# A GRU with a mixture of experts behind it: where the first block's gate inputs are summed, how the first seeds reach the gates, which engine adds the biases, and when zeros are copied

## The chip, the cores and the metric

The kernel runs on one core of a Trainium2 chip. The metric is the device time of one execution in microseconds. A core has five engines with queues of their own: TensorE (PE for its matmuls, PEld for its weight loads), VectorE (DVE), ScalarE (ACT), GpSimd (POOL) and SyncE (SP, which issues DMAs here). Each engine takes its instructions in program order; engines wait for one another, and for DMAs, by semaphores.

## The reference

The input x is [8, 256, 512], eight sequences of 256 steps. A GRU cell with a state of 512 goes over the steps, and a mixture of experts with a shared expert works on its outputs; x is added at the end. All in float32.

```python
def cell(h, x):
    gi = x @ W_ih + b_ih
    gh = h @ W_hh + b_hh
    i_r, i_z, i_n = jnp.split(gi, 3, axis=-1)
    h_r, h_z, h_n = jnp.split(gh, 3, axis=-1)
    r = jax.nn.sigmoid(i_r + h_r)
    z = jax.nn.sigmoid(i_z + h_z)
    n = jnp.tanh(i_n + r * h_n)
    h_new = (1.0 - z) * n + z * h
    return (h_new, h_new)
...
combine = jnp.sum(topk_w[..., None] * jax.nn.one_hot(topk_ids, E, dtype=x.dtype), axis=1)
gu = jnp.einsum('th,ehf->etf', x, w_gate_up)
act = _silu_and_mul(gu)
eo = jnp.einsum('eti,eih->eth', act, w_down)
routed = jnp.einsum('te,eth->th', combine, eo)
shared = _silu_and_mul(x @ w_sh_gate_up) @ w_sh_down
return (routed + shared).reshape(orig_shape)
```

There are 8 experts of width 256, of which each token takes 2, and the shared expert has a width of 1024.

## The kernel before

**Blocks and chunks.** The 256 steps are cut into 16 blocks of 16 steps (TS); a block holds 128 rows, 8 sequences by 16 steps. A block is cut into chunks of 4 steps (SC).

**The projections.** For block k and gate g (0 is r, 1 is z, 2 is n) `project(k, g)` makes four pieces, one for each quarter q of the contraction with W_ih. A piece is four matmuls with 512 columns each, which the trace shows as eight records of L338, `gip<-we,xT`. The sum of a gate stands in one PSUM bank. There are three such banks (`ps_mm`, handed out by `bank_of`), used in turn by projections, routing and the shared expert; whoever takes a bank first makes its old readers run, if they still stand in a queue (`held`). After the last piece `end()` brings the sum, plus the bias, into the tile `gi`. For block 0 one VectorE instruction does that (L430) into `gi_first`. For all other blocks ScalarE copies the bank into `gi_later` (L432) and GpSimd adds the bias there (L433). `gi_later` is a single tile with room for three gates of one block, so a gate's copy for block k+1 waits until the DMA that sends block k's values has read them. After gate z, the r and z columns are sent to DRAM (`gid_rz`, L441); after gate n, the n columns (`gid_n`, L443). Both sends are issued by SP. The sends of block 0 (`send_first`, L457 and L459, one for each chunk and kind) are issued by ACT.

**The seeds.** `load_seeds(c)` (L475) reads a chunk's gate inputs back from DRAM into `seeds` (r and z) and `seeds_n`, with partitions laid out as the gates need them; there are two buffers of each. `open_gate(n, g)` (L486, ACT) copies one step's seeds into the PSUM bank of the gate (`banks`, `gate_of`), and the recurrent matmuls add to it there. Chunk 0 is read by eight loads, four on ACT and four on POOL; every later chunk by eight loads on SP, issued after the last step of the chunk before the one that runs.

**A step.** `step(n)` issues the matmuls of r and n (32 records of L514 on `ps_rn`), then of z (32 on `ps_z`). VectorE turns r and n (L527), ACT takes the sigmoid of r (L531) and opens the next step's r and n gates, VectorE multiplies and adds (L534, L535), ACT takes the tanh (L537) and the sigmoid of z (L539) and opens the next z gate, VectorE forms the new state hT (L542, L544, L545), and ACT copies it to `hc` (L548). POOL copies one column of `hn` (L543); the next step's `hn` waits for that. Step n+1's matmuls need step n's hT and the opened gates.

**Between the steps.** Matmul work of other kinds is cut into pieces and put behind the matmuls of each step: projections of later blocks, the shared expert (`shared_unit`), routing. Each step may take 8 units of it (`PER_STEP`), a unit being four matmuls with 128 columns, or half of four with 256; what the routing uses is taken off. VectorE work of 0.66 to 1.1 us by the planner's own cost figures is put in a queue, `afterwards`, with its cost: the turn of a block's x (`transpose_x`, 1.1, L327), the shared expert's product (`weighted`, 0.9, L769 and L770), its final sum (`add_up`, 0.66). After each step `catch_up(room)` takes items from the front while their cost fits in the room: `WINDOW`, 1.1, less what the step's routing takes on VectorE (`busy` in the table `steps_`). If a consumer comes first, `needed()` runs every item up to the wanted one.

The routing of block k-1 runs in block k: `order_experts` in its step 2 (busy 1.2), `weigh` in 4 (1.0), `give_places` in 6 (1.2), `send_rows` in 8 (0.75, eight DMAs `rows<-hr` on SP), `read_rows` in 10 (`rb<-rows` on SP), each one step later in block 1, where `weigh_all` takes another 0.7 in step 6. The dealing of rows to experts (`deal_rows`, indirect DMAs on POOL) follows in steps 12 and 14. The DRAM tile `dealt` must hold zeros where no row is dealt: SP copies `blank` to it, eight DMAs of 256 KB in each block, one in each of steps 2 to 9.

**The head.** x_0 and three quarters of W_ih are queued on SP, then the two biases, the last quarter of W_ih, x_1, W_hh, x_2. TensorE turns x_0 (`turn_x_plain`), projects block 0 quarter by quarter over the three gates, turns x_1, runs ten pieces of block 1, and then step 0 is issued. POOL, after its constants, copies the hidden bias of n into both `seeds_n` tiles (L296).

**The tail.** After the 256 steps the rest of the shared expert and the experts' tiles run.

Of the kernel before, what the change touches and what calls it, by code (L numbers as in the profile page):

```python
# [17 lines left out]
P = 128  # L18
TS = 16
SC = 4  # L20
NS = 2
NH = 4


@with_exitstack
def kernel(
# [109 lines left out]
    for q in range(NQ):  # L136
        if q == NQ - 1:
            nc.sync.dma_start(bias, b_ih.partition_broadcast(P))
            nc.sync.dma_start(bias_h, b_hh[0 : 2 * D].partition_broadcast(P))
        nc.sync.dma_start(wih[:, q], w_ih.rearrange("(p q) n -> q p n", q=NQ)[q])  # L140
    load_x_plain(1)
    w_hh_v = w_hh.rearrange("(q p) n -> p q n", p=P)
# [147 lines left out]
    for j in range(4):  # L290
# [3 lines left out]
        )  # L294
    for tile_ in seeds_n:
        nc.gpsimd.tensor_copy(tile_, seed_hn.unsqueeze(1).broadcast_to([P, SC, P]))  # L296

# [12 lines left out]
    blank = dram.tile([P, D], F32, name="blank")  # L310
    load((dealt[E * NM], nothing), (blank, nothing))


# [91 lines left out]
    def project(k, g):  # L405

        box = {}

        def issue(q, cols):
            if q == 0 and cols.start == 0:  # L410
                if k in turned_x:
                    turned_x.pop(k)()
                box["ps"], _ = bank_of([P, D], f"gip_{k}_{g}")
            multiply(
                box["ps"][:, cols],
                lambda c: xT_of[k][:, c, q, :],
                wih[:, q, g * D + cols.start : g * D + cols.stop],
                start=(q == 0 and cols.start == 0),
                stop=(q == NQ - 1 and cols.stop == D),
            )  # L420

        def by_group(t_):
            return t_.rearrange("p (q j i) -> p j q i", q=NQ, j=4)

        def end():
            gi = gi_later if k else gi_first
            to_gi = gi[:, :, g, :].rearrange("p j (q i) -> p j q i", q=NQ)
            bias_g = by_group(bias[:, g * D : (g + 1) * D])
            if k == 0:
                nc.vector.tensor_tensor(to_gi, by_group(box["ps"]), bias_g, ALU.add)  # L430
            else:
                nc.scalar.copy(to_gi, by_group(box["ps"]))  # L432
                nc.gpsimd.tensor_tensor(to_gi, to_gi, bias_g, ALU.add)  # L433
            if g > 0:
                projected.add((k, "rzn"[g]))
            if g > 0 and k == 0:
                send_first(g, 0)
            elif g > 0:
                to = gi_dram[k][g % 2].rearrange("j b t n -> (b t) j n")
                if g == 1:  # L440
                    nc.sync.dma_start(to.rearrange("p j (a n) -> p j a n", a=2), gi[:, :, 0:2, :])  # L441
                else:
                    nc.sync.dma_start(to, gi[:, :, 2, :])  # L443

        return [
            matmul_piece(lambda cols, q=q: issue(q, cols), end if q == NQ - 1 else None)
            for q in range(NQ)
        ]

    projected = set()  # L450

    def send_first(g, c):
# [3 lines left out]
        if g == 1:  # L456
            nc.scalar.dma_start(to.rearrange("p j (a n) -> p j a n", a=2), gi_first[rows_, :, 0:2, :])  # L457
        else:
            nc.scalar.dma_start(to, gi_first[rows_, :, 2, :])  # L459

    def load_seeds(c, of="nz"):

        k, o = divmod(c * SC, TS)
        steps = slice(o, o + SC)
        for g in of:
            assert (k, g) in projected
            tile_, at_row = (seeds_n[c % NS], B) if g == "n" else (seeds[c % NS], 0)
            for j in range(4):
                if k:
                    src = gi_dram[k][int(g != "n")][j, :, steps, :]  # L470
                else:
                    src = gi_first_dram[int(g != "n")][o // SC, j].rearrange("t b n -> b t n")
                by = nc.sync if c else nc.scalar if g == "z" else nc.gpsimd
                row = 32 * j + at_row
                by.dma_start(tile_[row : row + B], src)  # L475

# [492 lines left out]
    nc.vector.transpose(states[0].rearrange("p q b -> p (q b)"), h.rearrange("p q i -> p (q i)"))  # L969
    nc.vector.tensor_tensor(bias[:, 0 : 2 * D], bias[:, 0 : 2 * D], bias_h, ALU.add)  # L970

    first = [project(0, g) for g in range(3)]
    for q in range(NQ):
        for g in range(3):
            first[g][q].run(None)
    catch_up(None)
    load_seeds(0, "z")
    load_seeds(0, "n")
    load_shared()

    projections = deque()
    for k in range(1, NB):
        for g in range(3):
# [6 lines left out]
    def turn_x_afterwards(k):  # L990
        turned_x[k] = afterward(1.1, lambda: transpose_x(k))

    turn_x_plain(1)
    ahead_of_it = 2 * NQ + 2
    while ahead_of_it:
        piece = projections.popleft()
        ahead_of_it -= piece.parts > 0
        piece.run(None)
    for g in gate_of:
        open_gate(0, g)  # L1000
    for c in range(1, TS // SC):
        for g in (1, 2):
            send_first(g, c)
    load_seeds(1)
    due = spent = 0.0
    to_enter = deque()
    for k in range(NB):
# [21 lines left out]
        for e in range(E):  # L1029
            when(2 + e, 0, 0, lambda k=k, e=e: nc.sync.dma_start(dealt[e * NM + k], blank))  # L1030
        if k > 1 and k % 2:
# [126 lines left out]
```

## Time and profile before

| what | us |
|---|---|
| median of 3 runs | 1397.16 |
| lowest, highest | 1394.51, 1398.63 |
| the profiled execution | 1394.11 |
| its span in the trace | 1391.9 |
| first matmul of step 0 | 32.07 |
| first matmul of step 1 | 37.76 |
| last step's matmuls | near 1141 |
| x is turned for block 1 on TensorE | 19.70 |
| bias sums on POOL (L433), 45 of them | 1.27 each |
| bias sums on VectorE for block 0 (L430), 3 | 0.69 each |
| VectorE turn of a block's x (L327), 14 | 1.15 each |

In the profile a line of the timeline has the start in us, the duration, engine, line, operation, what it writes and reads, and how often; in brackets is the idle time of its engine before it and what ended that. Lines of a waits view give who waited for whom, with us in total, times, and the longest. A q behind an engine's name means its sequencer, which issues DMAs.

### The profile page before, as it was taken

Reading aid. Unit: us, or ns where it says so; the run is one execution under the profiler, and the core shown is the slowest. Engines: PE = TensorE matmul, PEld = TensorE weight load, DVE = VectorE, ACT = ScalarE, POOL = GpSimd, SP = SyncE. Lnnn points to the kernel's source line nnn. Section 1 sums busy time; section 2 is a strip of 40 time slices with the busy share of each in tenths; the row PEclk is TensorE's granted clock in tenths of the full one; section 3 lists DMA queues with packets and bytes.
Section 4 is the critical chain, followed back from the end, with each engine's and each line's share of the span. In section 5 each row is a group of like instructions: output and inputs, shape, how many; then the busy total and the mean of one; then the engine's idle time right before and its main releaser. Section 6 shows DMA issues by size and latency. Waiting matters only on the chain. (4 is left out here: it accounts for less than half of the span.)

```text
span 1391.9 us, 58971 instructions
## 1 busy us (share of the span) xinstructions
PE 1369.2 (98%) x24512; PEld 781.5 (56%) x24512; DVE 653.6 (47%) x2701; ACT 473.5 (34%) x2037; POOL 291.2 (21%) x564
## 2 busy tenths in 40 slices
PE   8999999999999999999999999999999999999996
PEld 3455556665656565656665566566656655444442
DVE  2445444545454544455544554554445443344442
ACT  0444443434343434343434343434343330111111
POOL 3333432121111111111111111111111132133332
PEclk9999999999999999999999999999999999999999
DMA  8544563332332232223221322132223445455553
GB/s 269 169 138 147 125 125 108 112 107 90 97 100 67 74 83 75 67 82 83 81 76 59 83 83 82 59 87 78 67 67 90 127 112 154 91 93 102 94 102 50
DMA packets 94082, 137.62 MB, mean 99 GB/s; under 512 B 17256, under 2 KB 67864, under 8 KB 91768
## 3 DMA queue, kind: packets, MB, share of 16 engines
q1 hardware_dynamic: 77192, 95.54, 23.7%
q0 software_dynamic: 15152, 37.38, 11.8%
q8 instruction: 194, 3.18, 1.0%
q10 hardware_dynamic: 1472, 0.93, 0.3%
q14 instruction: 72, 0.59, 0.1%
HBM read 94.55 MB, written 72.78 MB: 120 GB/s over the span
## 5 line engine op out<-in xcount | busy, mean ns | idle before, releaser
L514 PE MATMUL ps_rn<-we,hT 128*8 128x256 f32 x8192 | 490.5, 379 | 5.6 <-DVE hT L545 2.7
L514 PEld LDWEIGHTS ps_rn<-we,hT 128*8 128x8 f32 x8192 | 223.3, 89 | 254.5 <-ACT ps_z L486 50.9
L527 DVE STREAM_TRANSPOSE rT<-ps_rn 128x128 f32<-128x128 f32 x256 | 81.1, 317 | 435.2 <-PE ps_rn L514 435.2
L514 PE MATMUL ps_z<-we,hT 128*8 128x128 f32 x8192 | 272.2, 273 | 0.0
L514 PEld LDWEIGHTS ps_z<-we,hT 128*8 128x8 f32 x8192 | 227.4, 90 | 50.8
L531 ACT ACTIVATE rT<-rT 128x32 f32<-128x32 f32 x256 | 58.5, 229 | 527.7 <-DVE rT L527 519.7
L543 POOL COPY last_hn<-hn 128x1 f32<-128x1 f32 x256 | 47.3, 185 | 825.6 <-DVE hn L542 825.6
L824 PE MATMUL gu_s<-hc,wsu 128*32 128x256 f32 x3072 | 188.4, 379 | 0.0
L338 PE MATMUL gip<-we,xT 128*32 128x512 f32 (+2 forms) x1872 | 185.7, 520 | 1.9 <-DVE xT L220 1.6
L824 PEld LDWEIGHTS gu_s<-hc,wsu 128*32 128x32 f32 x3072 | 101.0, 110 | 58.7 <-issue 11.8
L778 PE MATMUL gu_t<-we,xrT 128*128 x280 | 131.6, 593 | 1.8 <-issue 1.8
L338 PE MATMUL po<-wsd,act_s 128*32 128x512 f32 (+2 forms) x1272 | 130.2, 509 | 0.0
L338 PEld LDWEIGHTS gip<-we,xT 128*32 128x32 f32 x1872 | 59.7, 111 | 71.4 <-issue 60.4
L778 PEld LDWEIGHTS gu_t<-we,xrT 128*128 128x128 f32 x280 | 50.5, 190 | 52.9 <-issue 45.0
L527 DVE STREAM_TRANSPOSE zT<-ps_z 128x128 f32<-128x128 f32 x256 | 78.9, 308 | 0.0
L548 ACT COPY hc<-hT 128x32 f32<-128x32 f32 x192 | 47.4, 247 | 91.2 <-DVE hT L545 90.7
L486 ACT COPY ps_rn<-seeds_n 128x128 f32<-128x128 f32 x256 | 69.0, 270 | 8.2
L534 DVE TENSOR_TENSOR rT<-nT,rT 128x32 f32<-128x32 f32 x256 | 50.0, 195 | 42.6 <-ACT rT L531 42.2
L527 DVE STREAM_TRANSPOSE nT<-ps_rn 128x128 f32<-128x128 f32 x256 | 70.0, 273 | 0.0
L486 ACT COPY ps_rn<-seeds 128x128 f32<-128x128 f32 x256 | 68.9, 269 | 2.1 <-DMA seeds<-gid_rz_first 1.0
L914 DVE TENSOR_SCALAR y<-yp,share 128x512 f32<-128x512 f32 x35 | 26.2, 750 | 91.8 <-PE yp L911 72.8
L542 DVE TENSOR_TENSOR hn<-hT,rT 128x32 f32<-128x32 f32 x256 | 49.3, 193 | 38.7 <-ACT rT L537 11.2
(167 smaller groups left out, 1188.5 us busy)
## 6 DMA issues: line engine op xcount, KB each, us to landing
dealt<-blank SPq DMA_DIRECT2D x128, 256.0 KB
xr<-dealt SPq DMA_DIRECT2D x140, 64.0 KB
we<-in_L_ffn_w_gate_up_dram POOLq DMA_DIRECT2D x32, 256.0 KB, 4.4
gid_rz<-gi SPq DMA_DIRECT2D x15, 512.0 KB
seeds<-gid_rz SPq DMA_DIRECT2D x240, 32.0 KB
wsu<-_L_ffn_w_sh_gate_up_dram POOLq DMA_DIRECT2D x16, 256.0 KB, 3.8
rows<-hr SPq DMA_DIRECT2D x128, 32.0 KB
rb<-rows SPq DMA_DIRECT2D x16, 256.0 KB
```

Source lines behind the costliest of these rows:

```text
L338: nc.tensor.matmul(ps[32 * c : 32 * c + 32], lhs(c), rhs, start=start, stop=stop, skip_group_check=True,)
L486: nc.scalar.copy(gate_of[g], src)
L514: nc.tensor.matmul(banks[g][32 * j : 32 * j + B, 0 : n_ * P].rearrange("b (a k i) -> b a k i", a=n_, k=NQ), hT[:, q, 0:B], whh_v[:, q, j, ...
L527: nc.vector.transpose(gT.rearrange("p a b -> p (a b)"), gate_of[g])
L531: nc.scalar.activation(r, r, AF.Sigmoid)
L534: nc.vector.tensor_tensor(r, nT[:, :, 0:B], r, ALU.mult)
L542: nc.vector.tensor_tensor(hn, hT[:, :, 0:B], nn, ALU.subtract)
L543: nc.gpsimd.tensor_copy(last_hn, hn[:, 0, 0:1])
L548: nc.scalar.copy(hc_of_block(k).rearrange("p g q (c t) -> p q g c t", t=TS)[:, :, :, :, t], new.rearrange("p q (g c) -> p q g c", c=2),)
L778: nc.tensor.matmul(box["ps"], lhs(q), w_up(q), start=(q == 0), stop=(q == NQ - 1))
L824: nc.tensor.matmul(box["ps"][32 * g : 32 * g + 32, two_i, :], wsu[c][:, q, two_i, fs], hc_of[m][:, :, q, :], start=(two_i == 0 and q == 0) ...
L914: nc.vector.tensor_scalar(y, box["y"], laid["share"][:, i : i + 1], None, ALU.mult)
```

## The change

- Block 0's gate sums are built in the three gate banks (`rn`, `z`, `x`) in place of three of the `ps_mm` banks. VectorE still adds the bias into `gi_first`.
- Steps 0 and 1 (`NP = 2`) no longer get their seeds through DRAM. `pick`, a matrix of zeros and ones made by POOL from `ident`, picks their rows out of `gi_first` by 16 matmuls into the gate banks (`pick_seeds`, `first_seeds`); ACT copies r and z into `seeds[0]`, VectorE adds the hidden bias of n into `seeds_n[0]`.
- Steps 2 and 3 are still read back from DRAM. All eight sends of block 0 and these eight loads are issued by POOL, together, right after block 0's last projections.
- In the head, x_1 is loaded ahead of the biases and the last quarter of W_ih. The order on TensorE is: three quarters of block 0, turn of x_1, three quarters of block 1's r, last quarter of block 0, three quarters of block 1's z, the picks, block 1's last r quarter, three quarters of its n. The two pieces left over go to the front of the queue of the steps. POOL's copies into `seeds_n` come after its zeros and `pick`.
- For blocks 1 to 15 the bias is added by VectorE instead of POOL, and not at once: the sum is put in `afterwards` at a cost of 0.66, and the sends to DRAM go out when it runs. Before a gate's copy, a pending sum of the same gate is run.
- `turn_x_afterwards` rotates the queue by one, so that the turn of x comes to the front.
- The zero copies of a block move from steps 2 to 9 to pairs: two in each of steps 0, 1, 4 and 5 (in block 0: 4, 5, 8 and 9).

```diff
@@ -19,6 +19,7 @@
 TS = 16
 SC = 4
 NS = 2
+NP = 2
 NH = 4
 
 
@@ -135,10 +136,10 @@
     load_x_plain(0)
     for q in range(NQ):
         if q == NQ - 1:
+            load_x_plain(1)
             nc.sync.dma_start(bias, b_ih.partition_broadcast(P))
             nc.sync.dma_start(bias_h, b_hh[0 : 2 * D].partition_broadcast(P))
         nc.sync.dma_start(wih[:, q], w_ih.rearrange("(p q) n -> q p n", q=NQ)[q])
-    load_x_plain(1)
     w_hh_v = w_hh.rearrange("(q p) n -> p q n", p=P)
     for g in (0, 2, 1):
         cols = slice(g * D, (g + 1) * D)
@@ -292,8 +293,6 @@
             seed_hn[32 * j : 32 * j + B].rearrange("b (q i) -> b q i", q=NQ),
             b_hn[j].partition_broadcast(B),
         )
-    for tile_ in seeds_n:
-        nc.gpsimd.tensor_copy(tile_, seed_hn.unsqueeze(1).broadcast_to([P, SC, P]))
 
 
     rows = dram.tile([B, T, D], F32, name="rows")
@@ -309,6 +308,13 @@
     load((listed[0:P], vacant), (listed[P : E * NM + 1], vacant[0 : E * NM + 1 - P]))
     blank = dram.tile([P, D], F32, name="blank")
     load((dealt[E * NM], nothing), (blank, nothing))
+    pick = we[0 : SC * B, 2, 3, 0 : 6 * SC * B].rearrange("p (s m) -> p s m", s=SC)
+    nc.gpsimd.memset(pick, 0.0)
+    nc.gpsimd.tensor_copy(
+        pick[:, :, 2 * B : 3 * B], ident[0 : SC * B, 0 : SC * B].rearrange("p (s b) -> p s b", s=SC)
+    )
+    for tile_ in seeds_n:
+        nc.gpsimd.tensor_copy(tile_, seed_hn.unsqueeze(1).broadcast_to([P, SC, P]))
 
 
     spare = deque()
@@ -410,7 +416,10 @@
             if q == 0 and cols.start == 0:
                 if k in turned_x:
                     turned_x.pop(k)()
-                box["ps"], _ = bank_of([P, D], f"gip_{k}_{g}")
+                if k == 0:
+                    box["ps"] = banks[("rn", "z", "x")[g]]
+                else:
+                    box["ps"], _ = bank_of([P, D], f"gip_{k}_{g}")
             multiply(
                 box["ps"][:, cols],
                 lambda c: xT_of[k][:, c, q, :],
@@ -428,19 +437,24 @@
             bias_g = by_group(bias[:, g * D : (g + 1) * D])
             if k == 0:
                 nc.vector.tensor_tensor(to_gi, by_group(box["ps"]), bias_g, ALU.add)
+                if g > 0:
+                    projected.add((k, "rzn"[g]))
+                return
+            if g in biased:
+                biased.pop(g)()
+            nc.scalar.copy(to_gi, by_group(box["ps"]))
+            biased[g] = afterward(0.66, lambda: add_bias(to_gi, bias_g))
+
+        def add_bias(to_gi, bias_g):
+            nc.vector.tensor_tensor(to_gi, to_gi, bias_g, ALU.add)
+            if g == 0:
+                return
+            projected.add((k, "rzn"[g]))
+            to = gi_dram[k][g % 2].rearrange("j b t n -> (b t) j n")
+            if g == 1:
+                nc.sync.dma_start(to.rearrange("p j (a n) -> p j a n", a=2), gi_later[:, :, 0:2, :])
             else:
-                nc.scalar.copy(to_gi, by_group(box["ps"]))
-                nc.gpsimd.tensor_tensor(to_gi, to_gi, bias_g, ALU.add)
-            if g > 0:
-                projected.add((k, "rzn"[g]))
-            if g > 0 and k == 0:
-                send_first(g, 0)
-            elif g > 0:
-                to = gi_dram[k][g % 2].rearrange("j b t n -> (b t) j n")
-                if g == 1:
-                    nc.sync.dma_start(to.rearrange("p j (a n) -> p j a n", a=2), gi[:, :, 0:2, :])
-                else:
-                    nc.sync.dma_start(to, gi[:, :, 2, :])
+                nc.sync.dma_start(to, gi_later[:, :, 2, :])
 
         return [
             matmul_piece(lambda cols, q=q: issue(q, cols), end if q == NQ - 1 else None)
@@ -448,21 +462,22 @@
         ]
 
     projected = set()
+    biased = {}
 
     def send_first(g, c):
 
         rows_ = slice(SC * B * c, SC * B * (c + 1))
         to = gi_first_dram[g % 2][c].rearrange("j t b n -> (t b) j n")
         if g == 1:
-            nc.scalar.dma_start(to.rearrange("p j (a n) -> p j a n", a=2), gi_first[rows_, :, 0:2, :])
+            nc.gpsimd.dma_start(to.rearrange("p j (a n) -> p j a n", a=2), gi_first[rows_, :, 0:2, :])
         else:
-            nc.scalar.dma_start(to, gi_first[rows_, :, 2, :])
-
-    def load_seeds(c, of="nz"):
+            nc.gpsimd.dma_start(to, gi_first[rows_, :, 2, :])
+
+    def load_seeds(c):
 
         k, o = divmod(c * SC, TS)
-        steps = slice(o, o + SC)
-        for g in of:
+        steps = slice(o, o + SC) if c else slice(NP, SC)
+        for g in "nz":
             assert (k, g) in projected
             tile_, at_row = (seeds_n[c % NS], B) if g == "n" else (seeds[c % NS], 0)
             for j in range(4):
@@ -470,9 +485,35 @@
                     src = gi_dram[k][int(g != "n")][j, :, steps, :]
                 else:
                     src = gi_first_dram[int(g != "n")][o // SC, j].rearrange("t b n -> b t n")
-                by = nc.sync if c else nc.scalar if g == "z" else nc.gpsimd
                 row = 32 * j + at_row
-                by.dma_start(tile_[row : row + B], src)
+                if c:
+                    nc.sync.dma_start(tile_[row : row + B], src)
+                else:
+                    nc.gpsimd.dma_start(tile_[row : row + B, NP:], src[:, NP:])
+
+    def pick_seeds(s, gates, at, ps):
+
+        for j in range(4):
+            nc.tensor.matmul(
+                ps[32 * j : 32 * j + 32],
+                pick[:, s, at : at + 32],
+                gi_first[0 : SC * B, j, gates, :],
+                start=(s == 0),
+                stop=(s == NP - 1),
+                skip_group_check=True,
+            )
+
+    def first_seeds():
+        rz = banks["rn"].rearrange("p (s g n) -> p s g n", s=NP, g=2)
+        n = banks["x"][:, 0 : NP * P].rearrange("p (s n) -> p s n", s=NP)
+        for s in range(NP):
+            pick_seeds(s, slice(0, 2), 2 * B, rz[:, s])
+        for s in range(NP):
+            pick_seeds(s, slice(2, 3), B, n[:, s : s + 1])
+        nc.scalar.copy(seeds[0][:, 0:NP], rz.rearrange("p s g n -> p s (g n)"))
+        nc.vector.tensor_tensor(
+            seeds_n[0][:, 0:NP], n, seed_hn.unsqueeze(1).broadcast_to([P, NP, P]), ALU.add
+        )
 
     def open_gate(n, g):
 
@@ -967,19 +1008,9 @@
 
 
     nc.vector.transpose(states[0].rearrange("p q b -> p (q b)"), h.rearrange("p q i -> p (q i)"))
-    nc.vector.tensor_tensor(bias[:, 0 : 2 * D], bias[:, 0 : 2 * D], bias_h, ALU.add)
-
-    first = [project(0, g) for g in range(3)]
-    for q in range(NQ):
-        for g in range(3):
-            first[g][q].run(None)
-    catch_up(None)
-    load_seeds(0, "z")
-    load_seeds(0, "n")
-    load_shared()
 
     projections = deque()
-    for k in range(1, NB):
+    for k in range(2, NB):
         for g in range(3):
             projections.extend(project(k, g))
             if g == 0 and k + 1 < NB:
@@ -989,18 +1020,34 @@
 
     def turn_x_afterwards(k):
         turned_x[k] = afterward(1.1, lambda: transpose_x(k))
-
+        afterwards.rotate(1)
+
+    first, second = [[project(k, g) for g in range(3)] for k in range(2)]
+    for q in range(NQ - 1):
+        for g in range(3):
+            first[g][q].run(None)
     turn_x_plain(1)
-    ahead_of_it = 2 * NQ + 2
-    while ahead_of_it:
-        piece = projections.popleft()
-        ahead_of_it -= piece.parts > 0
-        piece.run(None)
+    for q in range(NQ - 1):
+        second[0][q].run(None)
+    nc.vector.tensor_tensor(bias[:, 0 : 2 * D], bias[:, 0 : 2 * D], bias_h, ALU.add)
+    for g in range(3):
+        first[g][NQ - 1].run(None)
+    for c in range(TS // SC):
+        for g in (1, 2):
+            send_first(g, c)
+    load_seeds(0)
+    load_shared()
+    for q in range(NQ - 1):
+        second[1][q].run(None)
+    first_seeds()
     for g in gate_of:
         open_gate(0, g)
-    for c in range(1, TS // SC):
-        for g in (1, 2):
-            send_first(g, c)
+    second[0][NQ - 1].run(None)
+    for q in range(NQ - 1):
+        second[2][q].run(None)
+    projections.extendleft(second[g][NQ - 1] for g in (2, 1))
+    catch_up(None)
+    turn_x_afterwards(2)
     load_seeds(1)
     due = spent = 0.0
     to_enter = deque()
@@ -1027,7 +1074,7 @@
             for i in range(2):
                 when(12 + late + 2 * i, 0, 0, lambda k=k, i=i: deal_rows(k - 1, i))
         for e in range(E):
-            when(2 + e, 0, 0, lambda k=k, e=e: nc.sync.dma_start(dealt[e * NM + k], blank))
+            when(e // 4 * 4 + e // 2 % 2 + 4 * (k == 0), 0, 0, lambda k=k, e=e: nc.sync.dma_start(dealt[e * NM + k], blank))
         if k > 1 and k % 2:
             for b in (3, 2):
                 when(6, 0, 0, lambda k=k, b=b: load_again(k - b))
```

## The prediction

> **What bounds the kernel now.** I read the busy shares first, then what TensorE waited for (us in total, times, longest), then the order of time in the head and at two later places.
>
> ```profile
> PE 1369.2 (98%) x24512; PEld 781.5 (56%) x24512; DVE 653.6 (47%) x2701; ACT 473.5 (34%) x2037; POOL 291.2 (21%) x564
> ```
>
> ```profile
> PE ps_rn L514 <- DVE hT L545: 2.7, 5, 1.2
> ...
> PE ps_rn L514 <- ACT ps_rn L486: 2.0, 1, 2.0
> ```
>
> TensorE is idle 1391.9 - 1369.2 = 22.7 us of the span, about 11 of them after its last work. All its waits with a name, those of the tail too, make 12.7 us, and the scan's part after 38 us is under 2. The chain that ended last is one entry long and says nothing here. So TensorE's own work is the bound, the change alters that work only by its picks, and it can win only idle time of the head. It can lose anywhere, because a step's chain is nearly as long as its TensorE work: in
>
> ```profile
> 32.07 1.91 PE L514 MATMUL ps_rn<-we,hT 128*8 128x256 f32 x32 [2.05 <-ACT ps_rn L486]
> 33.80 1.06 PE L514 MATMUL ps_z<-we,hT 128*8 128x128 f32 x32
> 34.67 1.90 PE L338 MATMUL gip<-we,xT 128*32 128x512 f32 x16
> 35.92 0.23 ACT L531 ACTIVATE rT<-rT 128x32 f32<-128x32 f32 x1 [3.71 <-DMA gid_rz_first<-we]
> 37.76 1.91 PE L514 MATMUL ps_rn<-we,hT 128*8 128x256 f32 x32 [1.19 <-DVE hT L545]
> ```
>
> step 0 begins at 32.07 after a wait for the seeds; its sigmoid is late because ACT's queue holds the sends of block 0 (the 3.71), and step 1 begins at 37.76, 5.69 later. A usual step takes 4.32 (154.64 to 158.96 below). From step 1 on any delay of a chain by more than about 0.1 us is paid in full.
>
> **The head.** Four matmul records of 512 columns start every 0.43 us (their weight loads stand at 25.12, 25.55, 25.97); a piece of a projection is eight records, 0.86 us; 80 records in 8.79 us say the same. The nine pieces on the first three quarters of W_ih end their issue at 16.46, as before. Then come, in the new order: the turn of x_1 to the first product, 1.53 (19.70 to 21.23 now); three pieces of block 1's r, three last pieces of block 0, three pieces of block 1's z, 9 x 0.857 = 7.7; the picks; four pieces more, 3.4. A pick's records: 16 of 256 columns and 16 of 128. By the rows above 32 of 256 take 33.80 - 32.07 = 1.73 and 32 of 128 take 34.67 - 33.80 = 0.87, so 0.86 + 0.43 = 1.3. Step 0 then starts at 16.46 + 1.53 + 7.7 + 1.3 + 3.4 = 30.4, and step 1, with ACT free of sends, at 34.7 instead of 37.76: **-3.0**. What must hide behind it: x_1, queued after three quarters of W_ih rather than after everything, is wanted at 16.5; the last quarter of W_ih, now 256 KB later (1 us at the slice's 269 GB/s, so 18.0 instead of 16.98), is wanted at 20.6; the DVE sums of block 0 (0.69 each) and the bias sum (1.18) run under block 1's z; the copies out of the banks (0.57, then three gates of 0.27) run under the last four pieces. Without that cover the sums and copies would cost about 3.
>
> The moved sends are eight DMAs on POOL and, behind them, eight loads of the seeds of steps 2 and 3. POOL's four DMAs at L291 took 2.47 together: 16 x 0.62 = 9.9 from 23.3, to 33.2, and a landing of 2.7 (the median of the seeds_n loads) makes 35.9. Step 1 copies them into the gate 2.57 after its start (40.33 against 37.76 now), at 37.3: hidden with 1.4 to spare. With the 6.3 us from send to first use that ACT's queue shows (19.70 to 25.98) they would be 2.2 late. What stands behind POOL's DMAs is the last_hn copy, for which DVE's next hn waits at 39: not late. So the head is worth between -3.5 (the 0.5 of the W_ih wait besides) and -0.8; I take -3.0.
>
> A change of matmul shape has a row: from the products to the turn of x_1 (19.15 to 19.70) it took 0.55 where a plain issue takes 0.43. Two such changes around the picks are 0.2, left out of the sum as below its rounding. The Trainium skill's page TensorEngine Tiling (Array Packing), section Key Properties, speaks against the picks: a change of tiling mode drains TensorE, and picks have 32 rows where the products have 128. No row here has that change of rows. With a whole drain on either side the head would win less, by the row 0.2 less.
>
> **The bias sums.** 45 sums leave POOL (1.27 each) for DVE. An SBUF sum of 1024 columns took 1.18 (L970), one of 512 from PSUM 0.69 (L430); DVE is idle 2.1 us between a step's hT and the next rT, so 0.69 inside that gap is free. POOL's sums also doubled a DVE product twice in the chain (L534 0.57 instead of 0.19 at 170.25; 0.39 at 131.19), after which steps came 0.35 and 0.14 late: **-0.5** when they go.
>
> But they are put in the queue of afterwards, one item to a step, none in a step whose own DVE work leaves less than its cost of 1.1. I worked the planner's arithmetic through for all 256 steps. For the code before, it puts all 45 gate copies, 14 turns of x, 12 final sums and the shared products in the steps where the trace has them, so I trust it for the code after. Two steps go wrong.
>
> First, **step 27**. In block 1 steps 21, 22, 23 and 25 are taken by routing, and 24 by the turn of x_6, which the new rotation sets in front. Block 5's r sum (copied in step 21) waits until 26, its z sum (copied in 23) until 27; only then is rz sent, by a DMA out of the single tile gi. Yet step 27 also copies block 6's r into the same columns. ACT must wait there for the landing, and everything of step 28 stands behind it in ACT's order: the sigmoid, three gates. Now the send has long gone, issued at 139.32:
>
> ```profile
> 147.07 5.10 SPq L673 DMA_DIRECT2D rows<-hr  x8
> ...
> 160.31 0.67 SPq L678 DMA_DIRECT2D rb<-rows  x1
> ```
>
> ```profile
> 154.64 0.58 ACT L432 COPY gi<-gip 128x512 f32<-128x512 f32 x1
> 157.03 0.23 ACT L531 ACTIVATE rT<-rT 128x32 f32<-128x32 f32 x1 [1.81 <-DVE rT L527]
> ```
>
> ```profile
> 154.64 1.92 PE L514 MATMUL ps_rn<-we,hT 128*8 128x256 f32 x32
> ...
> 158.96 1.27 PE L514 MATMUL ps_rn<-we,hT 128*8 128x256 f32 x20
> ```
>
> On this clock the sum would end at 154.48 + 0.69 = 155.2. In SP's order the rows, eight seeds and rb come ahead of the send. The packets of earlier rz sends ended 2.6 to 4.2 us after issue. Best case: 155.2 + 2.6 + copy 0.58 = 158.4 against the sigmoid's 157.03, 1.4 late. Worst: SP as far behind as now, 161.0 + 4.2 + 0.58 = 165.8, 8.7 late. Between: no zero copies or n send in the way, SP issues rb near 153.9; packets of rb took 4 to 6 us from issue in this and other blocks, so the send's own 2.5 us begin near 158.9 and end at 161.4; with the copy 162.0: **+5.0**, taken because it is nearest to the rows of this very place. The same check for every other reuse of gi leaves at least one whole step: block 1's rz, sent in step 1 and wanted in step 3, has some 1 us to spare, the rest 8 us and more.
>
> Second, **step 180**. Now:
>
> ```profile
> 814.88 0.42 DVE L769 TENSOR_TENSOR act_s<-gu_s,act_s 128x256 f32<-128x256 f32 x1
> ...
> 820.08 0.16 DVE L606 TENSOR_REDUCE gap<-gap 128x1 f32<-128x8 f32 x1
> ...
> 823.67 1.16 DVE L327 STREAM_TRANSPOSE xT<-x 128x512 f32<-128x512 f32 x1
> ```
>
> ```profile
> 817.72 1.91 PE L338 MATMUL gip<-we,xT 128*32 128x256 f32 x24
> 819.56 1.91 PE L514 MATMUL ps_rn<-we,hT 128*8 128x256 f32 x32
> ```
>
> The shared product (L769, L770) runs in step 179, the turn of x_14 in 181. The rotation swaps them. Then block 13's n projection wants the third bank back in step 180, its last reader has not run, and it is forced behind weigh: 820.24 + 0.06 + 0.83 = 821.1. TensorE has two of eight column parts (0.43) to do from 817.72, and waits from 818.15 to 821.2, then does six parts, 1.29, and starts step 181 at 822.5 instead of 819.56: **+2.9** (bounds 2.4 and 3.1; it can't be less, since TensorE's order is fixed).
>
> **Zero copies.** 128 DMAs of 256 KB move on SP from one a step (steps 2 to 9) to pairs in steps 0, 1, 4, 5. No TensorE or ACT wait after 45 us names them or the seeds they stood before: 0. They may now wait for the last dealing DMA of the block before (SP shows 16.0 us of such waits already); behind them stand the sends of gi and seeds with some 12 us of slack. If that cover went, each block could pay 1 us.
>
> **Sum.** -3.0 - 0.5 + 5.0 + 2.9 = **+4.4**. The profiled execution took 1394.11 (span 1391.9), the lowest end of the three runs, 3 us under their median; it would become 1398.5. Carried to the median of 1397.16: **1401.6**.
>
> The clock could make it worse. The first five fours of matmuls here ran at half pace until 10.9 us (0.86 us a four, then 0.43), 1.9 us lost in all; an idle of 2.05 at 30 us brought none of that back. A bound for the idle of step 28 is therefore 0 to 1.9; I take 0. The Trainium skill's page TensorE: Matmul & The Clock Gate, section What's actually happening, says that an idle window of about 3.4 us halves the clock. An idle of 5 us may or may not hold such a window whole; by that rule the sum would be up to 1.9 higher, by the row of 2.05 it is unchanged.
>
> **Rivals.** (1) The forecast, 0.58: 1398.6 to 1405.2, from the bounds 2 to 8.7 at step 27. (2) The landing at step 27 is quick (SP ahead, rb done): 1.4 instead of 5.0, sum +0.8, 1398.0; 0.13. For it: rows can start at 146.4 and SP loses eight other DMAs; against: rb never took under 4 us. (3) Both stalls come and the head gives nothing, or the clock falls: seeds 2 and 3 late by 2.2 or a cold stretch of 1.9, sum +6.3 to +7.4, about 1404; 0.17. (4) It gets faster: gi's reuse doesn't bite because ACT's copy need not wait or the sums run earlier than I count, and the turn of x_14 costs nothing, so the head's gain stands alone: -3.5, 1393.7, and up to 1.5 more where POOL's sums delayed sends: 1392.2. It decides once both stalls together cost under 3.5. Against it: the copies of a block's r do wait on the rz send's semaphore in this trace. 0.12.
>
> A measurement of this kernel can tell about 0.3%, 4.2 us, from no change. Slower by more: 0.38 of (1) and all of (3), 0.55. Within: 0.20 of (1), all of (2), 0.05 of (4), 0.38. Faster: 0.07. Range: 1394.5 (leaving out most of 4) to 1406.5 (3, with the upper bound of step 27 left out); (1) alone 1398.6 to 1405.2.
>
> **What will show it.** Step 0's first product near 30.4 and step 1 near 34.7, with 32 pick records before; DVE sums of 0.6 to 0.7 in the gaps, no POOL sums; one ACT wait of several us for the rz send at a gate copy 27 steps on, and TensorE waiting as long; one TensorE wait of 3 us before a projection near step 180, behind an act_s product. The prediction is wrong if gi's copies wait for nothing, if steps 1 to 3 wait for seeds, or if the scan's other steps lengthen.

## The result, and the profile after

The changed kernel takes 1401.99 us (median of 7 runs, 1400.66 to 1405.95) against 1396.81 for the kernel before on the same chip (7 runs, 1394.51 to 1398.63). The ratio is 1.0041, 95% interval 1.0032 to 1.0050: slower by 5.2 us, where 4.4 were forecast. The profiled execution took 1401.99 with a span of 1400.2; that of before, 1394.11, was faster than all 7 of these, so the two spans lie 8.3 apart.

The busy shares come first:

```profile
PE 1374.4 (98%) x24544; PEld 782.9 (56%) x24544; DVE 679.8 (49%) x2747; ACT 473.0 (34%) x2038; POOL 241.7 (17%) x533
```

POOL has lost 49.5 us and DVE has gained 26, as 45 sums moved. TensorE has 32 more matmuls, the picks, and 5.2 us more work; the picks are 1.4 of it. The rest is time in which the same matmuls took longer, a first sign of a lower clock.

To find the place, take the starts of the 256 steps (first matmul of `ps_rn`) in both traces and follow their distance:

| place | after minus before, us |
|---|---|
| up to the start of step 1 (35.67 against 37.76) | -2.09 |
| steps 1 to 27, together | +0.49 |
| step 28 takes 10.21 instead of 4.32 | +5.89 |
| step 29 takes 6.97 instead of 4.32 | +2.64 |
| steps 30 to 254, together | +0.48 |
| behind the start of step 255 | +0.9 |
| sum | +8.3 |

**The head.** Timeline of the changed kernel (start, length, engine, line, operation):

```profile
17.07 0.75 PE L219 MATMUL xTp<-ident,x 128*128 128x128 f32 x4
...
26.46 1.06 PE L497 MATMUL ps_rn<-we 32*32 32x256 f32 x16
27.35 0.62 PE L497 MATMUL ps_x<-we 32*32 32x128 f32 x16
27.60 0.59 ACT L513 COPY seeds<-ps_rn 128x512 f32<-128x512 f32 x1 [15.11 <-PE ps_rn L497]
...
27.90 3.64 PE L344 MATMUL gip<-we,xT 128*32 128x512 f32 x32
...
31.36 1.91 PE L555 MATMUL ps_rn<-we,hT 128*8 128x256 f32 x32
```

From the turn of x_1 (17.07) to step 0 is 14.29 us; the forecast had 30.4 - 16.46 = 13.9. The copies out of the banks (L513 is one) run under the 3.64 of projections, as intended, and step 1 follows 4.31 behind step 0 without the old wait. Most of what is missing lies ahead of 17.07: the nine pieces ended 0.6 later than in the trace of before, because the fours of matmuls came to full pace (0.43 us) at 11.8 us here and at 10.9 there.

**Step 28.** Timeline of the changed kernel, SP, ACT and PE:

```profile
152.39 0.67 SPq L719 DMA_DIRECT2D rb<-rows  x1
...
153.04 1.91 PE L555 MATMUL ps_rn<-we,hT 128*8 128x256 f32 x32
153.83 0.38 SPq L455 DMA_DIRECT2D gid_rz<-gi  x1
...
160.86 0.59 ACT L445 COPY gi<-gip 128x512 f32<-128x512 f32 x1 [7.69 <-DMA gid_rz<-gi]
161.34 0.23 ACT L572 ACTIVATE rT<-rT 128x32 f32<-128x32 f32 x1
...
163.24 3.60 PE L555 MATMUL ps_rn<-we,hT 128*8 128x256 f32 x32 [5.70 <-DVE hT L586]
```

This is the foreseen stall at the foreseen place. The send of block 5's r and z is issued at 153.83, right behind `rb`. The copy of block 6's r into the same tile waits for it until 160.86, a landing of 7.0 us. The sigmoid stands behind the copy, and TensorE waits 5.70 us at the end of that chain. But the products of step 29, 1.91 us elsewhere, then take 3.60 without any wait. The windows view (stretch, its length, busy time and count on PE, PEld, DVE, ACT and POOL, then granted TensorE clock, DMA share, GB/s) says why:

```profile
156.00:160.00 4.00, 1.54 (x24) 0.41 (x12) 0.00 (x0) 0.00 (x0) 0.00 (x0) 1.00 0.75 224
160.00:164.00 4.00, 0.76 (x8) 0.31 (x12) 1.90 (x7) 2.02 (x8) 0.82 (x2) 0.73 0.12 34
164.00:168.00 4.00, 4.00 (x56) 2.01 (x52) 1.28 (x5) 0.65 (x3) 0.38 (x1) 0.50 0.01 2
168.00:172.00 4.00, 4.00 (x72) 1.94 (x68) 1.38 (x5) 1.36 (x6) 1.19 (x2) 0.92 0.19 56
```

The granted clock is 0.50 from 161.8 to 168.6, 6.8 us. It falls 4.3 us after TensorE went idle, and the last 5.4 us of it fall on work. Half of these 5.4, 2.7, would be lost; step 29's excess is 2.64.

**Step 180** shows nothing of the foreseen 2.9. Timeline of the changed kernel:

```profile
825.56 1.91 PE L344 MATMUL gip<-we,xT 128*32 128x256 f32 x24
...
827.28 1.92 PE L555 MATMUL ps_rn<-we,hT 128*8 128x256 f32 x32
...
827.77 0.16 DVE L647 TENSOR_REDUCE gap<-gap 128x1 f32<-128x8 f32 x1
827.85 0.41 DVE L810 TENSOR_TENSOR act_s<-gu_s,act_s 128x256 f32<-128x256 f32 x1
```

The shared product (L810) is indeed pushed into step 180, directly behind `weigh` (L647 is its last on VectorE). But the projection at 825.56, which was to wait for it, had begun 2.3 us before it and waited for nothing.

### The profile page after: what moved, and what is told of

It is laid out like the page before. It is cut to its first block, busy times and chain, and to the rows that moved or that the text cites. A ratio compares the mean times of both kernels' runs of the same rounds, so it can differ in the third digit from the quotient of the medians.

```text
span 1400.2 us, 59018 instructions
## 1 busy us (share of the span) xinstructions
PE 1374.4 (98%) x24544; PEld 782.9 (56%) x24544; DVE 679.8 (49%) x2747; ACT 473.0 (34%) x2038; POOL 241.7 (17%) x533
## 5 line engine op out<-in xcount | busy, mean ns | idle before, releaser
L344 PE MATMUL gip<-we,xT 128*32 128x512 f32 (+3 forms) x1776 | 173.7, 512 | 0.8 <-DVE xT L221 0.8
L865 PEld LDWEIGHTS gu_s<-hc,wsu 128*32 128x32 f32 x3072 | 101.1, 110 | 58.6 <-issue 11.8
L344 PEld LDWEIGHTS gip<-we,xT 128*32 128x32 f32 x1776 | 56.3, 110 | 61.4 <-issue 52.5
```

Of the source, the lines that this page charges most:

```text
L344: nc.tensor.matmul(ps[32 * c : 32 * c + 32], lhs(c), rhs, start=start, stop=stop, skip_group_check=True,)
L865: nc.tensor.matmul(box["ps"][32 * g : 32 * g + 32, two_i, :], wsu[c][:, q, two_i, fs], hc_of[m][:, :, q, :], start=(two_i == 0 and q == 0) ...
```

## The experiments

Theory: the loss is the stall of block 5's send in step 28 plus the low clock behind it, and the head's gain stands beside it. Rivals: the head gives nothing; the put-off sums or their rotation cost all through the scan; the zero copies cause the stall. Ratios are to the kernel before on the same chip. "Offset" is the start of a step minus its start in before's trace. The kernel before takes 1394.5 to 1397.8 us from chip to chip, so a total that was expected in us is to be read as a ratio.

**e1: block 5 gets a tile of its own for its sums**, that of block 0, which is free by then.

```diff
-            gi = gi_later if k else gi_first
+            gi = gi_first if k in (0, 5) else gi_later
...
-            biased[g] = afterward(0.66, lambda: add_bias(to_gi, bias_g))
+            biased[g] = afterward(0.66, lambda: add_bias(gi, to_gi, bias_g))
```

The two sends in `add_bias`, not shown, read the same `gi`.

> The changed kernel, but block 5's gate inputs are gathered in the tile that block 0 used and left, so block 6's first gate copy overwrites nothing that is still being sent. Sums stay put off. Theory (the 10.21 and 6.97 us of steps 28 and 29 come from reusing the one gi tile under a send that is not done, and from the halved clock after it): both steps take 4.32 and step 28 no longer has an ACT wait for the rz send; 5.89 + 2.64 = 8.5 us less than the changed kernel, about 1393.5, a ratio to before of 0.9975. Rival (the DMA queues or VectorE are what is late at step 28, whoever waits): the wait shows under another name and at least half of the 8.5 stays, 1397 or more.

1390.55 us, ratio 0.9967 (0.9956 to 0.9978). Timeline of e1:

```profile
152.91 1.94 PE L555 MATMUL ps_rn<-we,hT 128*8 128x256 f32 x32
152.92 0.58 ACT L445 COPY gi<-gip 128x512 f32<-128x512 f32 x1
...
157.23 1.94 PE L555 MATMUL ps_rn<-we,hT 128*8 128x256 f32 x32
```

The copy that waited 7.69 now waits for nothing, and steps 28 and 29 take 4.32 each. The send is not quicker: issued at 153.39, its last packet ends 8.2 us later (6.5 in the changed kernel), but nothing waits for it. The span is 12.0 us under the changed kernel's. Steps 28 and 29 are 8.5 of that, as expected; 2.0 lie behind the start of step 255 and 1.5 in the other steps, which nothing here explains. One tile made the change slower rather than faster.

**e5: the stall kept, but TensorE kept busy in it.** Six products into an unused bank are added behind step 28's work; they are unused.

```diff
+            if n == 28:
+                for _ in range(6):
+                    multiply(banks["x"], columns(ident), wih[:, 0, 0:D], start=True, stop=True)
```

> The changed kernel with 24 matmuls of 512 columns added behind the pieces of step 28 (5.2 us of TensorE work into an unused bank, results unused), where TensorE now idles 5.70 us. Theory (step 29's 6.97 us is the clock that the idle time halved): step 28 still takes about 10.2, step 29 takes 4.32, the record of the granted clock has no half stretch in the scan, total 2.6 less than the changed kernel, 1399.4. Rival (step 29 is slow because its seeds, its weights or ACT's backlog are late): step 29 still takes near 7 and the total stays at 1402.

1399.12 us, ratio 1.0030 (1.0019 to 1.0042). Timeline of e5, then its window behind the stall:

```profile
157.31 5.34 PE L344 MATMUL ps_x<-we,ident 128*32 128x512 f32 x48
...
162.79 1.91 PE L555 MATMUL ps_rn<-we,hT 128*8 128x256 f32 x32
...
167.11 1.92 PE L555 MATMUL ps_rn<-we,hT 128*8 128x256 f32 x32
```

```profile
164.00:168.00 4.00, 4.00 (x91) 2.35 (x83) 2.31 (x9) 2.01 (x8) 0.66 (x2) 1.00 0.06 4
```

ACT waits 7.3 us for the send as before, and step 28 still takes 9.80. But the clock stays at 1.00 and step 29 takes 4.32. So the 2.64 of step 29 belong to the idle time, not to the wait: work without use, put into the idle stretch, took them away. The span is 4.8 under the changed kernel's, of which 2.64 are step 29; the two ratios alone overlap and would not show it.

**e4: the zero copies back in their old places** (one a step, in steps 2 to 9).

```diff
-            when(e // 4 * 4 + e // 2 % 2 + 4 * (k == 0), 0, 0, lambda k=k, e=e: nc.sync.dma_start(dealt[e * NM + k], blank))
+            when(2 + e, 0, 0, lambda k=k, e=e: nc.sync.dma_start(dealt[e * NM + k], blank))
```

> The changed kernel with the zero copies back in steps 2 to 9, one each. Theory (the rz send of block 5 lands the later, the more of SP's queue stands ahead of it): the wait at step 28 grows by 1 to 3 us, since three zero copies are again ahead of that send, total 1403 to 1405; all other steps unchanged. Rival (the new places of the zero copies cost something of their own in the blocks): step 28 the same within 0.5 us and the total under 1401.

1403.96 us, ratio 1.0068 (1.0052 to 1.0083). Timeline of e4, SP and ACT:

```profile
155.61 0.67 SPq L719 DMA_DIRECT2D rb<-rows  x1
...
156.38 0.39 SPq L455 DMA_DIRECT2D gid_rz<-gi  x1
...
161.73 0.58 ACT L445 COPY gi<-gip 128x512 f32<-128x512 f32 x1 [10.20 <-DMA gid_rz<-gi]
```

ACT waits 10.2 us for the send instead of 7.7, and step 28 takes 12.73. The send is issued 5.0 us after the start of step 28 instead of 0.8, and lands 5.4 us after issue instead of 7.0. So the new places don't cause the stall. That they shorten it is not shown: 2.5 us in these two traces, but the changed kernel's own step 28 took 11.86 in another execution (e11), and its ratio there, 1.0065, can't be told from e4's.

**e6: the kernel before with only the put-off sums and the rotation.** The head, the sends of block 0 and the zero copies are those of before. The sums and the later blocks' sends move into `add_bias`, as in the change; that part is not shown.

```diff
-                nc.scalar.copy(to_gi, by_group(box["ps"]))
-                nc.gpsimd.tensor_tensor(to_gi, to_gi, bias_g, ALU.add)
...
+            nc.scalar.copy(to_gi, by_group(box["ps"]))
+            biased[g] = afterward(0.66, lambda: add_bias(to_gi, bias_g))
...
+        afterwards.rotate(1)
```

> The kernel before with the put-off sums and the rotation alone: old head, zero copies in steps 2 to 9. Theory (the loss belongs to the put-off sums over the single gi tile, the head has no part in it): step 1 still starts near 37.8, step 28 takes 10 to 13 us and step 29 is slowed by the halved clock, together 7 to 10 us over before, about 1403 on the chip of the last runs. Rival (it needs the new head, which brings the sends of block 1 into the steps): no step over 5 us, within 2 us of before.

1409.59 us, ratio 1.0093 (1.0078 to 1.0109), 14 us where 7 to 10 were expected. ACT waits for the send twice, 18.0 us in all: for block 5 in step 28 (13.82) and for block 1 in step 3 (9.20). In the changed kernel block 1's reuse just fits; without the new head it doesn't. The granted clock is halved near 33, 53 and 169 us, for 3.4, 6.8 and 10.2 us.

**e3: the new head alone.** Sums at once on POOL, no rotation, old places of the zero copies.

```diff
-            biased[g] = afterward(0.66, lambda: add_bias(to_gi, bias_g))
+            add_bias(to_gi, bias_g)
...
-            nc.vector.tensor_tensor(to_gi, to_gi, bias_g, ALU.add)
+            nc.gpsimd.tensor_tensor(to_gi, to_gi, bias_g, ALU.add)
...
-        afterwards.rotate(1)
```

> The new head alone: biases summed by POOL at once as before, no rotation, zero copies in steps 2 to 9. Theory: step 1 starts near 35.7 instead of 37.76 and no step of the scan is over 5 us, total 2 to 3 us under before, a ratio of 0.998 to 0.9985. Rival (the head's gain is given back in steps 1 to 20, by SP's or POOL's later loads): step 1 early but step 32 at the time of before, a ratio of 1.000.

1394.25 us, ratio 0.9998 (0.9989 to 1.0008): 0.9980 to 0.9985 was expected; by the medians the head alone can't be told from nothing. Timeline of e3:

```profile
33.03 1.91 PE L555 MATMUL ps_rn<-we,hT 128*8 128x256 f32 x32
...
39.73 1.91 PE L555 MATMUL ps_rn<-we,hT 128*8 128x256 f32 x32 [2.21 <-DVE hT L586]
```

In this execution the matmuls had their full pace from 5.3 us on, and step 1 began 4.7 ahead of before. Then it took 6.71: ACT waited 1.7 us for the seeds of steps 2 and 3, POOL's last loads, and step 2 began at 39.73, hardly earlier than the 40.21 of the changed kernel with its slower start. POOL's first load had itself waited 3.4 us for block 0's sends to land. So POOL's loads bound step 2, and a faster start is partly lost there: with the same loads step 2 began at 38.88 in e8, where ACT waited 1.4 us for them, and at 38.36 in e4. In the scan e3 then loses another 1.3 by step 255.

**e7 and e9: that bound taken away**, in e1. ACT (e7) or SP (e9) issues the four loads of r and z that stand last on POOL. Shown is the edit of e9; e7 has `nc.scalar` there and issues them behind the first gates.

```diff
-                    nc.gpsimd.dma_start(tile_[row : row + B, NP:], src[:, NP:])
+                    by = nc.sync if g == "z" else nc.gpsimd
+                    by.dma_start(tile_[row : row + B, NP:], src[:, NP:])
```

> Block 5 in the other tile, and the r and z seeds of steps 2 and 3 loaded by ACT behind the first gates, those of n still by POOL: the eight loads no longer stand in one queue. Theory (what is left of the head's gain is bounded by these seeds: step 2 started at 40.2 with the change, at 38.4 to 39.7 where the clock rose early): step 1 takes 4.32 in every profile and the total is 0.2 to 2 us under the other tile alone, 1388.5 to 1390.3. Rival (ACT waits for the landing and holds up step 0's sigmoid): step 0 over 4.5 us, no gain.

> Block 5 in the other tile, and the r and z seeds of steps 2 and 3 loaded by SP, ahead of the seeds of chunk 1; those of n by POOL. Theory (the eight loads in one queue bound step 2, and only ACT's wait spoilt the split between ACT and POOL): steps 0 and 1 take 4.32 each, step 2 starts 8.64 after step 0, total 0.2 to 2 us under the other tile alone. Rival (the landing of block 0's own sends is what comes last, whoever loads): step 1 over 4.32 and no difference to the other tile alone beyond 0.5 us.

e7: 1393.72 us, ratio 0.9990 (0.9981 to 0.9999), worse than e1's, which it was to better. Step 1 no longer waits (4.53), but ACT's four issues stand ahead of step 0's sigmoid, and step 0 takes 5.15, 0.8 more than usual. Another 2.2 are lost between step 2 and step 255, without a cause that was found. e9: 1392.46 us, ratio 0.9970 (0.9958 to 0.9981). Steps 0 and 1 begin at 28.91 and 33.23, step 2 at 37.78, and ACT waits for no seeds, so the bound is gone, but the median is that of e1 within the interval.

**e2: sums on DVE, but at once, and no rotation.**

```diff
-            biased[g] = afterward(0.66, lambda: add_bias(to_gi, bias_g))
+            add_bias(to_gi, bias_g)
...
-        afterwards.rotate(1)
```

> The changed kernel with VectorE's sums made at once behind each gate's copy instead of put off, and without the rotation. Theory (putting off is what delays the rz send past block 6's copy): step 28 takes 4.32, total as with the other tile for block 5, near 1390.5 on the chip of the last runs, a ratio of 0.996 to 0.998. Rival (the sum meets other work of VectorE in the same gap, which is why it is put off): at least three steps lengthen by 0.5 us or more and the total is 2 us over that.

1394.83 us, ratio 0.9996 (0.9987 to 1.0005). The long stall is gone (step 28 takes 5.16), yet no gain is left: the offset goes from -2.72 at step 1 to -0.53 at step 255, 0.84 in step 28 and the rest in many pieces of 0.27; no other step is longer by 0.5. e1, with the sums put off and a free tile, is at 0.9967, but on another chip. On e2's chip the kernel nearest to e1 is e7, at 0.9990, and its interval overlaps that of e2 even with step 0's 0.8 us taken off. So it is not shown that putting the sums off is worth having.

**e8: e1 without the rotation.**

```diff
-        afterwards.rotate(1)
```

> Block 5 in the other tile, and no rotation, so that the turn of x_6 stands behind block 5's r sum. By the same arithmetic that named steps 27 and 180 the turn is then forced in step 25, just ahead of block 6's first product that needs it. Theory (a product that waits for forced VectorE work stalls TensorE): step 25 takes about 7.4 us, 3.0 more, everything else as with the other tile, near 1393.5. Rival (forced work costs nothing, as it turned out at step 180): no step over 5 us, 1390.5.

1394.37 us, ratio 0.9992 (0.9983 to 1.0001). Timeline of e8:

```profile
143.08 1.04 DVE L333 STREAM_TRANSPOSE xT<-x 128x512 f32<-128x512 f32 x1
...
144.27 1.96 PE L344 MATMUL gip<-we,xT 128*32 128x512 f32 x16 [2.66 <-DVE xT L333]
...
145.93 3.25 PE L555 MATMUL ps_rn<-we,hT 128*8 128x256 f32 x32
```

Without the rotation the turn of x_6 comes too late in the queue and is forced when its projection begins; TensorE waits 2.66 us for it (step 25 takes 7.54), and the clock halves for 3.4 us (step 26 takes 5.64). These 4.5 us are what the rotation saves once the sums are put off. By the medians it can't be told from e7 on the same chip.

**e10 and e11: e1 and the changed kernel again, on one chip**, beside e9.

> Block 5 in the other tile, once more, now on one chip with the changed kernel. Theory: 8 to 11 us under the changed kernel, a ratio to before of 0.9965 to 0.9985. Rival (the first measurement was a lucky head): within 0.1% of before, as the other versions of the head were.

> The changed kernel itself, on the same chip. Every theory: a ratio to before of 1.003 to 1.005, step 28 near 10 us and step 29 near 7, unless the halved clock of step 29 depends on where a free window happens to lie: then step 29 between 4.3 and 7.

e10: 1393.85 us, ratio 0.9965 (0.9952 to 0.9979). e11: 1406.42 us, ratio 1.0065 (1.0049 to 1.0080); step 28 takes 11.86 and step 29 5.97. The own tile is worth 12.6 us there, more than the 8 to 11 expected, and e1's first result was no lucky head. 9.2 of that are steps 28 and 29 in e11's trace.

**e12: the kernel before again**, to see how far one trace of it can be trusted.

> The kernel before, once more, as a control for the head. Theory: the head's start depends on when TensorE's first matmuls reach full pace, in the kernel before as in the others. If the fours of matmuls are at 0.43 us by about 6 us in this execution, step 0 begins near 29.6 in place of 32.07 and step 1 near 35.4 in place of 37.76, and the head alone (28.71, 33.03, step 2 at 39.73) would be ahead of it by only about 0 at step 2. If they reach full pace near 10.9 again, step 0 at 32.1 and step 1 at 37.8. Rival: the kernel before is held by its seeds and not by the pace, so that step 1 stays at 37.8 with an early pace too. The median is the same as before's, ratio 1.000 within 0.001.

1396.58 us, ratio 0.9999 (0.9990 to 1.0009). Timeline of e12:

```profile
16.42 2.78 PE L338 MATMUL gip<-we,xT 128*32 128x512 f32 x24 [1.98 <-DMA we<-in_L_cond_W_ih_dram]
...
31.56 2.75 PE L514 MATMUL ps_rn<-we,hT 128*8 128x256 f32 x32 [2.11 <-ACT ps_rn L486]
...
37.82 1.91 PE L514 MATMUL ps_rn<-we,hT 128*8 128x256 f32 x32
```

The rival holds: here the matmuls' pace was full by about 6 us, but the last quarter of W_ih (a wait of 1.98) and the seeds (2.11) held step 0, and ACT's sends step 1, at 37.82 as in the other trace. The clock fell to half for 3.4 us at step 0, hidden by those sends. Beyond step 1 the two traces of this one kernel drift apart by 2.0 us until step 255 (1.3 of it in steps 31 and 33).

## Why the prediction was right or wrong

**What bounds the kernel: right.** Each long delay of a chain was paid: 5.89 in the changed kernel and 3.2 in e8, each followed by the cost of a half clock, 2.64 and 1.3.

**Step 27/28: right in place and cause, sized 5.0 where it measured 5.89** (7.5 in e11). The planner's arithmetic, worked for each step, found the one reuse of 15 that bites; e1 removes it and the loss with it. SP's order was as the case "between" assumed, with the send soon after `rb`. The term mis-sized was the time from `rb`'s issue to the send's landing: 7.5 us (153.9 to 161.4) in the estimate, 8.5 (152.39 to 160.86) in the trace. With 7.0 to 8.9 us from issue to landing in two executions of one kernel, the spread of the landing alone, 1.9, is larger than the error of 5.0.

**The clock: wrong, 0 taken, 2.64 measured**, above the bound of 1.9 too. The step that failed reads from "an idle of 2.05 at 30 us brought none" to "I take 0": one idle that cost nothing says nothing of an idle nearly three times as long. In e12, the same kernel, an idle of 2.11 in the same place was followed by a half clock of 3.4 us. The bound failed as it was the loss of one start-up; the half clock lasted 6.8 us. The Trainium skill's page TensorE: Matmul & The Clock Gate, section What's actually happening, gives the half clock as the state after at least one idle window of about 3.4 us. The half clocks here last 3.4, 6.8 and 10.2 us, multiples of such a window, and the idle of 5.70 brought one, which agrees. But idles of 2.66 (e8) and 2.11 (e12), shorter than the window, were followed by one too, where 2.21 in e3 and 2.05 in before were not; the measurement decides, and what tells these apart stays open.

**Step 180: wrong, 2.9 taken, 0 measured.** The queue's arithmetic was right: the rotation pushes the shared product behind `weigh` in step 180. What failed is "block 13's n projection wants the third bank back". The prediction took it that banks are handed out in strict turn; the trace has the projection start without a wait 2.3 us ahead of the product, so that product did not hold it up. That it had another bank, one free for longer, is an inference.

**The head: -3.0 taken, -2.1 measured in this trace**, within its bounds of -3.5 to -0.8; other executions with the new head had step 1 up to 4.8 ahead (e8) and step 2 1.9 to 4.3 ahead. 0.4 of the miss is in the pieces from the turn of x_1 on (the picks 1.44 instead of 1.3, the turn of x_1 1.53 as taken, the rest in changes of shape), the other 0.6 ahead of it, in the later full pace. That POOL's seed loads are "hidden with 1.4 to spare" held only for a start as late as this one; in e3 they were 1.7 late, in e8 1.4. The sum of 16 issues had nothing for the loads' wait until the sends land, 1.0 us here and 3.4 in e3. The picks began 0.15 behind the sum of the pieces before them and took 0.14 more than worked out, so the drain at a change of tiling mode, of which the Trainium skill's page TensorEngine Tiling (Array Packing), section Key Properties, speaks, cost no more than 0.3 here.

**The zero copies: 0 taken; not contradicted.** The ratios with the new and the old places, 1.0065 (e11) and 1.0068 (e4), can't be told apart. Whether the places bear on the length of the stall stays open: its step took 10.21 and 11.86 with the new ones, 12.73 with the old.

**The bias sums, -0.5: not shown.** No step can be pointed to, and two traces of before drift by 2.0 over the scan. Sums put off, with the rotation and a free tile (e1, 0.9967), came out better than sums at once on DVE (e2, 0.9996) and, in the head-only kernel, on POOL (e3, 0.9998). Only e1 and e3 ran on one chip, and they differ in more than the sums, so the sums' own share stays open.

**The total** was right by luck: errors cancelled. In the spans, 4.4 were forecast and 8.3 came: step 180 took 2.9 away; head (0.9), stall (0.9), clock (2.6), sums (0.5), and scan and tail (1.9) added 6.8. The medians lie only 5.2 apart, since the profiled execution of before was quicker than all its other runs (1394.11 against a median of 1396.81), and so the forecast's 4.4 looks better than its parts. Rival 3's cold stretch was part of what happened; rival 4's -3.5 is about what e1 has, -3.9 and -4.0 by the medians.

**Open:** an extra 1 to 2 us near steps 36 to 39 in e4, e6, e8, e10 and e11 that the changed kernel's first trace doesn't have (TensorE stands idle there for 1.1 us in e4 and 1.8 in e11 and waits for nothing that the profile shows), and why e2 and e7 lose 2.2 over the scan.

**The better version** is e1: block 5's sums in the tile of block 0, ratio 0.9967 and 0.9965 on two chips; e9's loads on SP add nothing that can be told. That e7, which differs from it by four issues, came to 0.9990 on a third chip is a reason not to take this gain of 4 us for granted.

## What to carry to other kernels

When work that reads or sends a tile is put off, list for each use of the tile which step the put-off reader really runs in and which instruction overwrites the tile next; in an engine that works in order, one such overwrite holds everything behind it, and a second tile for that one use can be worth the whole change. On a kernel bound by TensorE, price an idle of 2 to 6 us with the half clock that may follow, and test it by filling the idle with unused work. Before explaining differences of 1 or 2 us that are spread over a long loop, profile the same kernel twice.

## What the hardware showed that was not expected

- After idles of 2.11 (e12), 2.66 (e8) and 5.70 us (the changed kernel) the granted clock was 0.50 for 3.4, 3.4 and 6.8 us; idles of 2.05 in another execution of before and of 2.21 in e3 brought none. The price was 2.64 us for the longest, 1.3 in e8.
- One 512 KB send, issued 1.4 us behind a 256 KB read of `rows`, landed after 7.0 us, and after 8.9 in another execution (e11). By its packets it ended 6.5 us after issue, where such sends in the trace of before, from block 3 on, took 2.6 to 4.2.
- The first matmuls reach full pace at about 5 to 6, at 10.9 or at 11.8 us from one execution to the next, with the same code (e12 against before), and step 0 of the new head began at 28.67 (e8) to 31.36 us (the changed kernel).
